# Second mixture of experts: outputs scattered from slots to tokens instead of gathered by token, and the last batch routed in the attention's stage

## The chip, the core and the metric

The kernel runs on one core of a Trainium2 chip. A core has five engines with a queue of instructions each: TensorE (PE in the profile, its weight loads PEld), VectorE (DVE), ScalarE (ACT), GpSimd (POOL) and SyncE (SP). Each engine takes its instructions strictly in order. Transfers are issued by SP, by ACT and, where the rows are chosen by an index tile, by POOL; all of them run on the core's 16 DMA engines. The metric is the device time of the core in microseconds, the median of several runs.

## The reference, cut to what matters

The input is x with 8 batches of 512 tokens of 128 numbers, 4096 tokens in all. There are two layers, each `x = x + s * silu(g)` over a layer norm of x. In the first, s is a state-space block (a scan over time for 16 states and 256 channels) and g a mixture of 24 experts with two matmuls each. In the second, s is a causal attention with 8 heads of width 128, and g is the second mixture, which this change is about:

```python
logits = xt @ wg                      # 4096 tokens, 128 experts
gates = softmax(logits)
e1, e2 = the two best experts         # loc1, loc2: the token's place in each one's list
g1, g2 = g1 / (g1 + g2), g2 / (g1 + g2)
v1, v2 = loc1 < 32, loc2 < 32         # an expert has 32 places; later comers are dropped
buf[e1 * 32 + loc1] += xt * v1        # second choices come behind all first choices
buf[e2 * 32 + loc2] += xt * v2
yb = einsum('ecd,edf->ecf', buf, we)  # one 128x128 matmul for each expert
y = (g1 * v1) * yb[place of e1] + (g2 * v2) * yb[place of e2]
```

A token that is dropped by an expert gets nothing from it.

## The kernel before

All instructions are written in Python loops. A scheduler then sets each engine's order: it takes ready instructions by their place in the program, and lets later ones go ahead while earlier ones wait. Semaphore waits follow from which tiles (also those in DRAM) an instruction reads and writes. Tiles with the same tag share a fixed number of buffers, so a new tile waits until an old one is released.

**The stages.** First come the preparation of x, the routing of the first mixture, and its experts; the scan runs beside them in steps (`step`, 64 in all, each two of the 16 states of one batch, with `front` and `back` for what goes in and comes out). Then the *early* attention stage follows: batches 0 to 5, 8 heads each, 48 in all (`early`), with the scan's remaining steps spread evenly over the 48. `back(b)` writes `s_dram[b]`, which `fetch(b)` loads; `after(b, ...)` makes the second layer's input of it, and `Attention.prepare(b, xb)` the layer norm, the logits, the two best experts, the attention's input and, in `route`, the places.

**Routing.** For each token and choice k the index `e * 32 + place` goes into `idx1` (a dropped token gets a spare row past 4096). Each batch has four tiles of 128 tokens, and each tile is stored twice by an indirect DMA of POOL (line 831), into `xs_dram[0]` for the first choice and `xs_dram[1]` for the second. Both tables were filled with zeros near the start of the program (line 415).

**The late stage.** When the early heads and the scan are through, their pools are given up and new ones are opened, PSUM among them. In program order there follow batch 7's `after` and `prepare`, `weights2` (weights of all tokens), `places` (which slots of the second choice's half hold a token: `live`, from the expert counts), and then batches 6 and 7's heads. Between these 16 heads stand the second mixture's pieces: `slots(t)` loads 512 slots of each table and transposes them; `experts(e0, ...)` does eight experts' matmuls, multiplies by `live` and stores the slots' outputs into `yb_dram` (line 979); and `finish(b)` for batches 0 to 5. Batches 6 and 7's `finish` comes at the end. `finish(b)` loads s1 and x1, gathers for each of four token tiles the rows of the first and second expert (lines 991 and 992, through the helper at line 127), weights and adds them (lines 993 and 994), and stores the result. Batches of s1, x1 and y have two buffers each; the gathered rows share six; the experts' output `yb` has three.

The lines that the change and the prediction speak of most:

```python
G.indirect_dma_start(xs_dram[k][:, :], IOA(idx1[:, b * NJ + j, k : k + 1], 0), xn2[:, j, :], None)   # 831
V.tensor_tensor(yb, py, bc(live[:, e0 // 2 : e0 // 2 + 4].unsqueeze(2), (P, 4, D)), ALU.mult)        # 978
Q.dma_start(rows(yb_dram[2 * C1 * e0 : 2 * C1 * (e0 + 8), :]), yb)                                   # 979
```

Other lines named: 605 to 608 are the scan on VectorE, 629 its transposes on TensorE; 849 to 863 a head's scores and exponentials (859 adds the mask and takes the minimum), 877 to 895 its values.

Of the kernel before, what the change touches and what calls it, by code (L numbers as in the profile page):

```python
# [20 lines left out]
P = 128  # L21
# [11 lines left out]
S1 = E1 * C1  # L33
HEADS, DHEAD = 8, 128
# [12 lines left out]
def tile_kernel(ctx: ExitStack, tc: tile.TileContext, t: dict, out: bass.AP):  # L47
# [42 lines left out]

    xs_dram = [dram.tile([S1 + P, D], F32, name=f"xs_dram{k}") for k in range(2)]
    yb_dram = dram.tile([2 * S1, D], F32, name="yb_dram")

# [75 lines left out]
    w121 = w3.tile([P, NTT, 2], F32, name="w121")  # L169
    row1 = w3.tile([P, NTT, 2], I32, name="row1")  # L170
    idx1 = w3.tile([P, NTT, 2], I32, name="idx1")
    kp1 = w3.tile([P, NTT, 2], F32, name="kp1")
# [22 lines left out]
    zero = inv_pool.tile([P, L], F32, name="zero")  # L195
    G.memset(zero, 0.0)
# [140 lines left out]
    def routing():  # L337
# [75 lines left out]
        for k in range(2):  # L413
            tc.keep_in_program_order(
                Q.dma_start(
                    xs_dram[k][0:S1, :].rearrange("(p n r) d -> p n (r d)", p=P, r=L // D),
                    bc(zero.unsqueeze(1), (P, S1 // L, L)),
                )
            )
# [323 lines left out]
    class Attention:  # L743
# [6 lines left out]
        def prepare(self, b, xb):  # L750

            at, (ps_x, px) = self.at, self.ps_x
            xn2 = at.tile([P, NJ, D], F32, name="xn2", bufs=1)
            layernorm(st, xb, xn2, NJ, eps5, "ln1")
            pt = ps_x.tile([P, L], F32, name="pt2", tag=px)
            for j in range(NJ):
                T.transpose(pt[:, j * P : (j + 1) * P], xn2[:, j, :], ident)
# [12 lines left out]
            V.tensor_tensor(lg, lg, bc(mx1[:, bs, 0:1], (P, NJ, E1)), ALU.subtract)  # L770
            S.activation(lg, lg, AF.Exp)
            V.tensor_reduce(se1[:, bs], lg, AX.X, ALU.add)

            sq = at.tile([P, NJ, D], F32, name="sq2", bufs=1)
            ss = st.tile([P, NJ], F32, name="ss2")
            for j in range(NJ):
                S.activation(sq[:, j, :], xn2[:, j, :], AF.Square, accum_out=ss[:, j : j + 1])
# [4 lines left out]
            V.tensor_tensor(sq, xn2, bc(ss.unsqueeze(2), (P, NJ, D)), ALU.mult)  # L782
            pt = ps_x.tile([P, L], F32, name="pt3", tag=px)
            for j in range(NJ):
                T.transpose(pt[:, j * P : (j + 1) * P], sq[:, j, :], ident)
            xaT = at.tile([P, L], F32, name="xaT", bufs=3)
            S.activation(xaT, pt, AF.Copy, scale=gamma)
            self.route(b, xn2)
            return xaT

        def route(self, b, xn2):
# [28 lines left out]
            kp = kp1[:, bs, :]  # L820
# [5 lines left out]
            for k in range(2):  # L826
                V.tensor_scalar(pos[:, :, k], pos[:, :, k], float(C1 - 1), float(k * C1), ALU.min, ALU.add)
            V.scalar_tensor_tensor(row1[:, bs, :], e12, float(2 * C1), pos, ALU.mult, ALU.add)
# [87 lines left out]
    def weights2():  # L916
        V.reciprocal(se1, se1)
        V.tensor_tensor(w121, mx1[:, :, 0:2], bc(mx1[:, :, 0:1], (P, NTT, 2)), ALU.subtract)
        S.activation(w121, w121, AF.Exp)
        V.tensor_tensor(w121, w121, bc(se1.unsqueeze(2), (P, NTT, 2)), ALU.mult)  # L920
        den = r3.tile([P, NTT], F32, name="den1")
        V.tensor_tensor(den, w121[:, :, 0], w121[:, :, 1], ALU.add)
        V.tensor_scalar(den, den, EPS32, None, ALU.max)
        V.reciprocal(den, den)
        V.tensor_tensor(w121, w121, bc(den.unsqueeze(2), (P, NTT, 2)), ALU.mult)
        V.tensor_tensor(w121, w121, kp1, ALU.mult)

    def places():


        pair = r3.tile([P, 2], F32, name="pair")
# [19 lines left out]
        V.tensor_scalar(live, pk, c, float(C1), ALU.add, ALU.is_lt)  # L951


    def slots(t):
        for k in range(2):
            xg = mo.tile([P, 4, D], F32, name="xg1", bufs=4)
            Q.dma_start(xg, rows(xs_dram[k][t * L : (t + 1) * L, :]))
            px = ps_x.tile([P, 4, P], F32, name="pxs", tag="px")
            for j in range(4):
                T.transpose(px[:, j, :], xg[:, j, :], ident)  # L960
# [11 lines left out]
    def experts(e0, we):  # L972
# [6 lines left out]
        Q.dma_start(rows(yb_dram[2 * C1 * e0 : 2 * C1 * (e0 + 8), :]), yb)  # L979

    def finish(b):
# [4 lines left out]
        y = mo.tile([P, NJ, D], F32, name="y", tag="y")  # L986
# [78 lines left out]
    for n, of in mixture():  # L1065
        due += n / of
        while due > 0.5:
            step()
            due -= 1.0
    moe.close()  # L1070
# [22 lines left out]
    def early():  # L1093
        for b in range(EARLY):
# [33 lines left out]
    live = r3.tile([P, E1 // 2], F32, name="live")  # L1128
    loaded = {e0: load_experts(e0) for e0 in range(0, 32, 8)}
# [21 lines left out]
    for b in range(EARLY):  # L1151
        second.append([lambda b=b: finish(b)])
# [5 lines left out]
    for b in range(EARLY, B):  # L1158
# [67 lines left out]
```

## Time and profile before

| | |
|---|---|
| three runs | 1612.73, 1624.30, 1623.59 us; median 1623.59 |
| the profiled execution | 1646.25 us |
| its span, first to last instruction | 1644.5 us |
| mean granted TensorE clock | 0.866 |
| busy: TensorE matmul, VectorE, ScalarE, GpSimd | 1243.5, 1256.5, 986.1, 588.6 us |
| indirect DMAs of POOL in routing (line 831) | 64, 1248 ns mean |
| last scan transposes (line 629) | 1376 us |
| last `s_dram` store of the scan (line 703) | 1421 us |
| routing of the last batch, scatters | 1459.8 to 1469.6 us |
| expert outputs `yb` (line 978) | 1478.2 to 1533.3 us |
| gathers of `finish` | 1536.3 to 1636.5 us |

A profile is one execution; its durations and its span belong together, and its own time is above the median of the runs. A row of a timeline has the start, the time it took, the engine, the line, the operation with output and inputs by name, and in brackets how long the engine stood idle before it and what ended that. A row of a table of stretches has a stretch, its length, each engine's busy time with its number of instructions, the granted clock, the DMA engines' busy share and GB/s. The chain of waits goes back from the last instruction to whatever released it.

### The profile page before, as it was taken

What the parts mean: (1) busy time and instruction counts of PE and PEld (TensorE: products, weight loads), DVE (VectorE), ACT (ScalarE), POOL (GpSimd) and SP (SyncE); (2) the same over time, 40 slices, a digit from 0 to 9 for tenths busy, and PEclk for the clock granted to TensorE, in tenths of its full rate; (3) what the DMA queues carried; (4) which work ended last, traced back from release to release, by engine and by line L of the source; (5) the groups of instructions that cost most, each with busy time, mean ns of one, the idle gap of its engine ahead of it and who ended that gap; (6) DMA issues with size and microseconds to landing.
All of it is one profiled execution on the core that took longest, in us unless ns stands there. A gap on an engine that the chain in (4) does not pass through costs nothing.

```text
span 1644.5 us, 20522 instructions
## 1 busy us (share of the span) xinstructions
PE 1243.5 (76%) x6797; PEld 873.5 (53%) x6797; DVE 1256.5 (76%) x2831; ACT 986.1 (60%) x1696; POOL 588.6 (36%) x502
## 2 busy tenths in 40 slices
PE   4787989311389988174888998889898899889764
PEld 2654455101377886151465665656656667567443
DVE  6558687679847866695999999999989896475454
ACT  2226778557567786364677768758567574552442
POOL 2016653565264440722253405730521111010455
PEclk9887999655589999576899999989989899999886
DMA  4438987677567863423142412421321200439133
GB/s 137 150 112 288 302 286 227 218 239 229 167 194 252 269 188 124 121 84 83 55 108 64 110 64 63 95 90 60 78 65 52 81 29 14 104 104 256 53 109 93
DMA packets 170668, 222.76 MB, mean 135 GB/s; under 512 B 15722, under 2 KB 115898, under 8 KB 170562
## 3 DMA queue, kind: packets, MB, share of 16 engines
q1 hardware_dynamic: 125634, 101.35, 19.8%
q10 hardware_dynamic: 18432, 67.12, 12.4%
q0 software_dynamic: 26496, 52.98, 12.1%
q8 instruction: 54, 0.88, 0.2%
q14 instruction: 52, 0.43, 0.1%
HBM read 163.52 MB, written 57.80 MB: 135 GB/s over the span
## 4 chain that ended last, share of the span: by engine, by line
PE 35%; DVE 33%; DMA 10%; issue 9%; ACT 7%; POOL 5%; another core or an unknown queue 1%; ACTq 0%; SPq 0%; DVEq 0%; POOLq 0%
DVE u L607 8%; PE po L884 5%; PE sc L857 4%; DVE u L605 4%; DVE u L608 4%; DVE sc L859 3%; PE py L629 3%; PE ph L453 2%; DMA hd<-hs_dram,row 2%; PE po L520 2%; DMA os_dram<-os 2%; DVE s L895 2%; PE pp L877 2%; PE pc L561 2%; PE pv L842 2%
## 5 line engine op out<-in xcount | busy, mean ns | idle before, releaser
L607 DVE TENSOR_TENSOR_SCAN u<-da,u 128x512 f32<-128x512 f32 x256 | 311.5, 1238 | 67.5 <-ACT da L603 47.9
L629 PE MATMUL py<-ident,u 128*128 128x128 f32 x1024 | 171.2, 306 | 159.7 <-DVE u L608 159.4
L629 PEld LDWEIGHTS py<-ident,u 128*128 128x128 f32 x1024 | 135.8, 158 | 201.1 <-DVE u L608 176.0
L884 PE MATMUL po<-v,pT 128*128 128x129 f32 x1280 | 189.1, 291 | 40.2 <-DVE s L895 27.0
L884 PEld LDWEIGHTS po<-v,pT 128*128 128x128 f32 x1280 | 171.3, 203 | 73.6 <-issue 29.8
L603 ACT ACTIVATE da<-dt,a_neg 128x512 f32<-128x512 f32 x256 | 175.7, 720 | 53.7 <-DVE u L607 51.5
L863 ACT ACTIVATE prob<-sc,mn 128x128 f32<-128x128 f32 (+3 forms) x256 | 130.5, 528 | 112.3 <-DVE mn L859 97.8
L857 PE MATMUL sc<-xaT,qm 128*128 128x128 f32 (+3 forms) x512 | 180.2, 461 | 13.8 <-ACT prob L863 9.9
L605 DVE TENSOR_TENSOR u<-bb,lp 128x1024 f32<-128x1024 f32 x128 | 155.0, 1228 | 16.0 <-DMA bb<-xd_dram 16.0
L608 DVE TENSOR_TENSOR u<-u,cb 128x1024 f32<-128x1024 f32 x128 | 158.1, 1235 | 1.1
L859 DVE CUSTOM_DVE_ANT_0 sc<-sc,mask 128x128 f32<-128x128 f32 (+3 forms) x256 | 125.2, 497 | 35.9 <-PE sc L857 28.1
L831 POOL DMA_INDIRECT xs_dram<-xn,idx x64 | 79.9, 1248 | 162.4 <-DVE idx L825 110.3
L877 PE MATMUL pp<-ident,prob 128*128 128x128 f32 x640 | 113.5, 286 | 30.6 <-DVE pT L879 19.7
L127 POOL DMA_INDIRECT xg<-xn_dram,inv x72 | 89.5, 1243 | 131.0 <-DVE lp L584 78.8
L130 POOL DMA_INDIRECT o<-os_dram,row x64 | 114.1, 1783 | 46.8 <-DMA o<-xn_dram 29.0
L877 PEld LDWEIGHTS pp<-ident,prob 128*128 128x128 f32 x640 | 80.8, 146 | 93.5 <-issue 43.1
L127 POOL DMA_INDIRECT hg<-hid_dram,inv x72 | 88.5, 1230 | 104.9 <-PE pht L515 51.5
L857 PEld LDWEIGHTS sc<-xaT,qm 128*128 128x128 f32 x512 | 82.8, 198 | 51.7 <-ACT prob L863 26.7
L127 POOL DMA_INDIRECT hd<-hs_dram,row x64 | 76.1, 1189 | 80.2 <-DMA bb<-xd_dram 31.6
L879 ACT COPY pT<-pp 128x384 f32<-128x384 f32 (+1 forms) x93 | 48.0, 516 | 57.8 <-PE pp L877 41.4
L520 PE MATMUL po<-we,hgT 128*128 128x128 f32 x576 | 79.7, 288 | 0.3 <-ACT hgT L517 0.3
L520 PEld LDWEIGHTS po<-we,hgT 128*128 128x128 f32 x576 | 72.3, 199 | 14.0 <-issue 9.8
(293 smaller groups left out, 2595.6 us busy)
## 6 DMA issues: line engine op xcount, KB each, us to landing
bb<-xd_dram ACTq DMA_DIRECT2D x64, 512.0 KB
cb<-xd_dram ACTq DMA_DIRECT2D x64, 512.0 KB
hs_dram<-hs SPq DMA_DIRECT2D x24, 768.0 KB
we<-in_W SPq DMA_DIRECT2D x48, 256.0 KB
hid_dram<-hd SPq DMA_DIRECT2D x32, 256.0 KB
we<-in_we SPq DMA_DIRECT2D x16, 512.0 KB
os_dram<-os SPq DMA_DIRECT2D x24, 192.0 KB
xb<-in_x SPq DMA_DIRECT2D x16, 256.0 KB
```

The source lines that it names most:

```text
L127: G.indirect_dma_start(dst, None, table[:, :], IOA(idx, 0))
L520: T.matmul(po[:, c, :], hT[:, f, :], we[:, f, :], start=False, stop=(f == NJ - 1))
L603: S.activation(da[:, j, :], dt[:, hf, :], AF.Exp, scale=a_neg[:, hf, n0 + j : n0 + j + 1])
L605: V.tensor_tensor(u, bb, bc(dx[:, hf : hf + 1, :], (P, NC, L)), ALU.mult)
L607: V.tensor_tensor_scan(u[:, j, :], da[:, j, :], u[:, j, :], 0.0, ALU.mult, ALU.add)
L608: V.tensor_tensor(u, u, cb, ALU.mult)
L629: T.matmul(py[:, i, hf * P : (hf + 1) * P], us[hf][:, j, i * P : (i + 1) * P], ident, is_transpose=True, start=False, stop=(n0 + j == DS - ...
L857: T.matmul(sc[:, :w], qm[:, i * P : w], xaT[:, :w], start=True, stop=True)
L859: V.tensor_tensor_reduce(sc[:, :w], sc[:, :w], mask[:, L - w :], -1.0, FMAX, ALU.add, ALU.min, mn[:, i : i + 1])
L863: S.activation(pr, sc[:, :w], AF.Exp, bias=mn[:, i : i + 1], scale=-1.0)
L877: T.transpose(pp[:, c, :], prob[i][:, k * P : (k + 1) * P], ident)
L884: T.matmul(po[:, i - i0, :], pT[:, i * (i + 1) // 2 + k, :], v[:, k, hd % 4, :], start=(k == 0), stop=(k == i),)
```

## The change

- The rows of both `xs_dram` tables grow from 128 to 132 numbers: behind the token's data stand, for each choice, its weight and its row in the output (`home`). They are filled not with zeros alone but with a spare output row for empty slots.
- `prepare` works out the batch's two weights itself (`weights2` goes) and puts them and `home` behind the normalised token, so that `route`'s scatters carry them along. `route` no longer computes the gather's rows.
- `places` loads weights and rows back from the tables by slot, multiplies `live` with the weights, and keeps the rows in `to`.
- `experts` stores its four tiles of slots by four indirect DMAs of POOL, straight to the tokens' rows of `y_dram`, which has one half for each choice. 16 calls make 64 of them. `y_dram` is filled with zeros behind the first mixture.
- `finish(b)` loads both halves' 512 rows and adds them; all eight `finish` come behind all heads.
- The scan's remaining steps are spread over 42 of the early heads, not 48, and batch 7's `fetch`, `after` and `prepare` are put between the last of the 48.

```diff
-    xs_dram = [dram.tile([S1 + P, D], F32, name=f"xs_dram{k}") for k in range(2)]
-    yb_dram = dram.tile([2 * S1, D], F32, name="yb_dram")
+    xs_dram = [dram.tile([S1 + P, DX], F32, name=f"xs_dram{k}") for k in range(2)]     # DX = D + 4
+    y_dram = dram.tile([2 * NY, D], F32, name="y_dram")                                # NY = NTOK + P
...
+    home_i = w3.tile([P, NTT + 1, 2], I32, name="home_i")
+    G.iota(home_i, pattern=[[P, NTT + 1], [NY, 2]], base=0, channel_multiplier=1)
...
-                    xs_dram[k][0:S1, :].rearrange("(p n r) d -> p n (r d)", p=P, r=L // D),
-                    bc(zero.unsqueeze(1), (P, S1 // L, L)),
+                    xs_dram[k][0:S1, :].rearrange("(p n) d -> p n d", p=P),
+                    bc(empty[:, k : k + 1, :], (P, S1 // P, DX)),
...
         def prepare(self, b, xb):
...
+            V.reciprocal(se1[:, bs], se1[:, bs])
+            w12 = st.tile([P, NJ, 2], F32, name="w121")
+            V.tensor_tensor(w12, mx1[:, bs, 0:2], bc(mx1[:, bs, 0:1], (P, NJ, 2)), ALU.subtract)
+            S.activation(w12, w12, AF.Exp)
+            V.tensor_tensor(w12, w12, bc(se1[:, bs].unsqueeze(2), (P, NJ, 2)), ALU.mult)
+            den = st.tile([P, NJ], F32, name="den1")
+            V.tensor_tensor(den, w12[:, :, 0], w12[:, :, 1], ALU.add)
+            V.tensor_scalar(den, den, EPS32, None, ALU.max)
+            V.reciprocal(den, den)
+            more = xn2[:, :, D:].rearrange("p j (k a) -> p j k a", a=2)
+            V.tensor_tensor(more[:, :, :, 0], w12, bc(den.unsqueeze(2), (P, NJ, 2)), ALU.mult)
+            V.tensor_copy(more[:, :, :, 1], home[:, bs, :])
...
         def route(self, b, xn2):
...
-            for k in range(2):
-                V.tensor_scalar(pos[:, :, k], pos[:, :, k], float(C1 - 1), float(k * C1), ALU.min, ALU.add)
-            V.scalar_tensor_tensor(row1[:, bs, :], e12, float(2 * C1), pos, ALU.mult, ALU.add)
...
     def places():
+        more = r3.tile([P, E1 // 2, 2], F32, name="more")
+        for a in range(2):
+            for k in range(2):
+                h = 2 * C1 * a + C1 * k
+                Q.dma_start(
+                    more[h : h + C1], xs_dram[k][0:S1, D + 2 * k : D + 2 * k + 2].rearrange(
+                        "(q a c) d -> a c q d", a=2, c=C1)[a]
+                )
...
+        V.tensor_tensor(live, live, more[:, :, 0], ALU.mult)
+        V.tensor_copy(to, more[:, :, 1])
...
     def experts(e0, we):
...
-        Q.dma_start(rows(yb_dram[2 * C1 * e0 : 2 * C1 * (e0 + 8), :]), yb)
+        for j in range(4):
+            q = e0 // 2 + j
+            G.indirect_dma_start(y_dram[:, :], IOA(to[:, q : q + 1], 0), yb[:, j, :], None)
...
     def finish(b):
...
-        for j in range(NJ):
-            i = b * NJ + j
-            ya = mo.tile([P, D], F32, name="ya", tag="row", bufs=6)
-            yc = mo.tile([P, D], F32, name="yc", tag="row", bufs=6)
-            gather(ya, yb_dram, row1[:, i, 0:1])
-            gather(yc, yb_dram, row1[:, i, 1:2])
-            V.tensor_scalar(ya, ya, w121[:, i, 0:1], None, ALU.mult)
-            V.scalar_tensor_tensor(y[:, j, :], yc, w121[:, i, 1:2], ya, ALU.mult, ALU.add)
+        y = mo.tile([P, NJ, D], F32, name="y")
+        Q.dma_start(y, rows(y_dram[b * L : (b + 1) * L, :]))
+        y2 = mo.tile([P, NJ, D], F32, name="y2")
+        Q.dma_start(y2, rows(y_dram[NY + b * L : NY + (b + 1) * L, :]))
+        V.tensor_tensor(y, y, y2, ALU.add)
...
+    for k in range(2):
+        tc.keep_in_program_order(
+            Q.dma_start(
+                y_dram[k * NY : k * NY + NTOK, :].rearrange("(p n) d -> p n d", p=P),
+                bc(empty[:, 0:1, 0:D], (P, NTOK // P, D)),
+            )
+        )
     moe.close()
...
     total = EARLY * HEADS
+    done = total - 6
...
-        while (taken - (NSTEP - left)) * total < (i + 1) * left:
+        while (taken - (NSTEP - left)) * done < (i + 1) * left and taken < NSTEP:
             step()
+        if i == done - 1:
+            for _ in model_steps:
+                pass
+        if i == done + 1:
+            got = fetch(B - 1)
+        if i == done + 2:
+            xb = after(B - 1, *got)
+            ready[B - 1] = beside.prepare(B - 1, xb)
...
-    for b in range(EARLY + 1, B):
-        ready[b] = last.prepare(b, after(b, *fetch(b)))
-    weights2()
     places()
...
-    for b in range(EARLY):
-        second.append([lambda b=b: finish(b)])
...
-    for b in range(EARLY, B):
+    for b in range(B):
         finish(b)
```

More of the change, by code (lines that the diff above doesn't have):

```diff
@@ L33 @@
 S1 = E1 * C1
+DX = D + 4
+NY = NTOK + P
 HEADS, DHEAD = 8, 128
@@ L168, in tile_kernel @@
     e121 = w3.tile([P, NTT, 2], F32, name="e121")
-    w121 = w3.tile([P, NTT, 2], F32, name="w121")
-    row1 = w3.tile([P, NTT, 2], I32, name="row1")
+    home = w3.tile([P, NTT + 1, 2], F32, name="home")
+    home_i = w3.tile([P, NTT + 1, 2], I32, name="home_i")
+    G.iota(home_i, pattern=[[P, NTT + 1], [NY, 2]], base=0, channel_multiplier=1)
+    V.tensor_copy(home, home_i)
     idx1 = w3.tile([P, NTT, 2], I32, name="idx1")
-    kp1 = w3.tile([P, NTT, 2], F32, name="kp1")
     cnt = w3.tile([NTT, 2, E1], BF16, name="cnt")
@@ L194, in tile_kernel @@
     bias = inv_pool.tile([3 * 32, DH + D], BF16, name="bias")
-    zero = inv_pool.tile([P, L], F32, name="zero")
-    G.memset(zero, 0.0)
+    empty = inv_pool.tile([P, 2, DX], F32, name="empty")
+    G.memset(empty, 0.0)
+    for k in range(2):
+        G.tensor_copy(empty[:, k, D + 2 * k + 1 : D + 2 * k + 2], home[:, NTT, k : k + 1])
     pick = inv_pool.tile([3 * 32, E0], BF16, name="pick")
@@ L752, in prepare @@
             at, (ps_x, px) = self.at, self.ps_x
-            xn2 = at.tile([P, NJ, D], F32, name="xn2", bufs=1)
-            layernorm(st, xb, xn2, NJ, eps5, "ln1")
+            xn2 = at.tile([P, NJ, DX], F32, name="xn2", bufs=1)
+            layernorm(st, xb, xn2[:, :, 0:D], NJ, eps5, "ln1")
             pt = ps_x.tile([P, L], F32, name="pt2", tag=px)
             for j in range(NJ):
-                T.transpose(pt[:, j * P : (j + 1) * P], xn2[:, j, :], ident)
+                T.transpose(pt[:, j * P : (j + 1) * P], xn2[:, j, 0:D], ident)
             xT = at.tile([P, L], F32, name="xT2", bufs=1)
@@ L776, in prepare @@
             for j in range(NJ):
-                S.activation(sq[:, j, :], xn2[:, j, :], AF.Square, accum_out=ss[:, j : j + 1])
+                S.activation(sq[:, j, :], xn2[:, j, 0:D], AF.Square, accum_out=ss[:, j : j + 1])
             V.tensor_scalar(ss, ss, 1e-24, None, ALU.max)
@@ L781, in prepare @@
             V.tensor_scalar(ss, ss, float(D) ** 0.5, None, ALU.mult)
-            V.tensor_tensor(sq, xn2, bc(ss.unsqueeze(2), (P, NJ, D)), ALU.mult)
+            V.tensor_tensor(sq, xn2[:, :, 0:D], bc(ss.unsqueeze(2), (P, NJ, D)), ALU.mult)
             pt = ps_x.tile([P, L], F32, name="pt3", tag=px)
@@ L819, in route @@
                 V.tensor_reduce(pos[:, j0 : j0 + 2, :], pm, AX.X, ALU.add)
-            kp = kp1[:, bs, :]
+            kp = st.tile([P, NJ, 2], F32, name="kp1")
             V.tensor_scalar(kp, pos, float(C1), None, ALU.is_lt)
@@ L913, in heads @@
                 yield
[L916 to L926, printed above, removed]
-    def places():
+    def places():
+        more = r3.tile([P, E1 // 2, 2], F32, name="more")
[6 more added lines that the diff above has]
+                )
         pair = r3.tile([P, 2], F32, name="pair")
@@ L951, in places @@
         V.tensor_scalar(live, pk, c, float(C1), ALU.add, ALU.is_lt)
+        V.tensor_tensor(live, live, more[:, :, 0], ALU.mult)
+        V.tensor_copy(to, more[:, :, 1])
     def slots(t):
         for k in range(2):
-            xg = mo.tile([P, 4, D], F32, name="xg1", bufs=4)
+            xg = mo.tile([P, 4, DX], F32, name="xg1", bufs=4)
             Q.dma_start(xg, rows(xs_dram[k][t * L : (t + 1) * L, :]))
@@ L959, in slots @@
             for j in range(4):
-                T.transpose(px[:, j, :], xg[:, j, :], ident)
+                T.transpose(px[:, j, :], xg[:, j, 0:D], ident)
             dst, src = xsT[:, 16 * t : 16 * t + 16, k, :], px.rearrange("p j (e c) -> p (j e) c", c=C1)
@@ L985, in finish @@
         Q.dma_start(x1, rows(x1_dram[b][:, :]))
-        y = mo.tile([P, NJ, D], F32, name="y", tag="y")
-        for j in range(NJ):
-            i = b * NJ + j
-            ya = mo.tile([P, D], F32, name="ya", tag="row", bufs=6)
-            yc = mo.tile([P, D], F32, name="yc", tag="row", bufs=6)
-            gather(ya, yb_dram, row1[:, i, 0:1])
-            gather(yc, yb_dram, row1[:, i, 1:2])
-            V.tensor_scalar(ya, ya, w121[:, i, 0:1], None, ALU.mult)
-            V.scalar_tensor_tensor(y[:, j, :], yc, w121[:, i, 1:2], ya, ALU.mult, ALU.add)
+        y = mo.tile([P, NJ, D], F32, name="y")
[3 more added lines that the diff above has]
+        V.tensor_tensor(y, y, y2, ALU.add)
         S.activation(y, y, AF.Silu)
@@ L1069, in tile_kernel @@
             due -= 1.0
+    for k in range(2):
+        tc.keep_in_program_order(
[4 more added lines that the diff above has]
+        )
     moe.close()
@@ L1128, in tile_kernel @@
     live = r3.tile([P, E1 // 2], F32, name="live")
+    to = r3.tile([P, E1 // 2], I32, name="to")
     loaded = {e0: load_experts(e0) for e0 in range(0, 32, 8)}
     last = Attention(at, m_qk, w_vo, (ps_x, "px"), (ps_q, "pq"), (ps_s, "ps"), (ps_t, "pt"), (ps_o, "po"))
-    for b in range(EARLY + 1, B):
-        ready[b] = last.prepare(b, after(b, *fetch(b)))
-    weights2()
     places()
```

## The prediction, made before the changed kernel ran

> **What bounds the kernel now.** The program has stages with different limits, so I read the table of stretches before anything else. The first stretch is the stage in which the scan shares the engines with the attention; the others cut what follows at the last scan work (1376), the first late head (1423), the last scatter of the routing (1471) and the last expert output (1533).
>
> ```profile
> core 0: us, PE busy (x) PEld busy (x) DVE busy (x) ACT busy (x) POOL busy (x), PEclk, DMA share, GB/s
> 790.00:1376.00 586.00, 525.19 (x2823) 365.28 (x2821) 554.01 (x1399) 411.33 (x705) 183.19 (x130) 0.94 0.24 70
> 1376.00:1423.00 47.00, 40.19 (x199) 26.07 (x198) 21.63 (x73) 23.38 (x49) 9.05 (x10) 0.96 0.08 23
> 1423.00:1471.00 48.00, 43.10 (x217) 28.65 (x216) 30.91 (x129) 27.90 (x57) 10.25 (x10) 0.96 0.51 133
> 1471.00:1533.00 62.00, 58.69 (x514) 45.42 (x513) 37.10 (x99) 21.39 (x42) 0.13 (x1) 1.00 0.72 204
> 1533.00:1645.00 112.00, 62.20 (x278) 43.91 (x276) 52.34 (x181) 42.73 (x66) 62.68 (x64) 0.76 0.32 90
> ```
>
> Up to 1376 VectorE is the bound: 554.0 of 586 us, 94.5%. After that no engine is full, so waits decide. How many attention heads each stretch holds is read from the mask-and-minimum line, L859, at 8 instructions a head:
>
> ```profile
> core 0: us, DVE busy (x), PEclk, DMA share, GB/s
> 790.00:1376.00 586.00, 98.99 (x368) 0.94 0.24 70
> 1376.00:1423.00 47.00, 5.20 (x20) 0.96 0.08 23
> 1423.00:1471.00 48.00, 10.33 (x38) 0.96 0.51 133
> 1471.00:1533.00 62.00, 10.54 (x38) 1.00 0.72 204
> 1533.00:1645.00 112.00, 13.32 (x48) 0.76 0.32 90
> ```
>
> That is 46, 2.5, 4.75, 4.75 and 6 heads. From 1376 to 1423 only two and a half remain from the early list, since the late heads need PSUM that the last `back` still holds. From 1423 a head takes 10.1 us; from 1471, with the experts between, 13.1; from 1533 about 17, since six batches' gathers sit in the same in-order queues. The waits and the chain of the end name what the last stretch hangs on:
>
> ```profile
> POOL ya L127 <- DMA yb_dram<-yb: 64.9, 1, 64.9
> 1533.30 2.27 DMA yb_dram<-yb
> ...
> 1635.60 3.06 DMA yc<-yb_dram,row
> ```
>
> The gathers start when the last expert's store has landed; the very last gather needs 3.06 us to land and is followed by 6 us of `finish`.
>
> **The row that decides the change** is the routing's scatter, L831, the only indirect store in the trace:
>
> ```profile
> 1310.30 1.86 POOL L831 DMA_INDIRECT xs_dram<-xn,idx  x1 [0.59 <-DVE rsum L889]
> 1312.47 0.97 POOL L831 DMA_INDIRECT xs_dram<-xn,idx  x1 [0.30 <-issue]
> 1315.50 1.02 POOL L831 DMA_INDIRECT xs_dram<-xn,idx  x1 [2.06 <-DMA xs_dram<-xn,idx]
> 1317.52 0.96 POOL L831 DMA_INDIRECT xs_dram<-xn,idx  x1 [1.01 <-DMA xs_dram<-xn,idx]
> ...
> 1461.05 0.97 POOL L831 DMA_INDIRECT xs_dram<-xn,idx  x1 [0.30 <-issue]
> 1462.32 0.96 POOL L831 DMA_INDIRECT xs_dram<-xn,idx  x1 [0.30 <-issue]
> 1463.59 0.95 POOL L831 DMA_INDIRECT xs_dram<-xn,idx  x1 [0.30 <-DMA xs_dram<-xn,idx]
> ```
>
> They alternate between two tables. The third waits until the first has landed, the fourth for the second: a scatter into a table waits for the scatter before it into the same table, since nobody knows the rows in advance. With two tables this hides at quiet times (1461.05 to 1463.59 is 2.54 us, two issues of 1.27). In the busy group it does not: 1310.30 to 1315.50 is 5.20, 1312.47 to 1317.52 is 5.05. The change sends all 64 output scatters into one table, `y_dram`, so every one waits for its predecessor.
>
> **Step 1, the scan stage.** The scan's steps are spread over 42 heads, not 48, so at its end six heads fewer are done, and batch 6's `after` and `prepare` still lie ahead. A head costs VectorE, by its groups over 64 heads, (125.2 + 36.5 + 68.6 + 9.8 + 58.4 + 21.1 + 21.0) / 64 = 5.3 us of summed durations, about 4.3 net because neighbours overlap; six are 26 us. `prepare` plus `after` is 14 us net (four 128x512 passes of 0.69, maxima and indices 2.4, masks 1.4, positions 3.1, two layer norms 4.5). So 40 us / 0.945 = 42 us earlier. Against it:
> - Eight small VectorE instructions more in each `prepare`, three fewer in `route`, each about 0.08 us net (0.16 by duration): 0.5 us for each of five batches, 2.5 us, on the bound engine. The eight exponentials go to ScalarE, 70% busy here: nothing, or 1.28 us for each table load they cause (ends 0 and 10 us; I take 0, as another exponential stands just before).
> - Two zero fills of `y_dram`, 4.2 MB of 512-byte rows on SP's queue at the start of the attention, where VectorE waits for the first gather-adds. At 306 GB/s (the best 20 us of such rows, 1480 to 1500) they take 14 us. All hidden is 0, none hidden 14; I take 4, as POOL's issue paces the gather-adds.
> - `xs_dram`'s fill in 528-byte pieces, not 2 KB: bounds -1 and 3 us, beside mixture work at 115 us; I take 2. The two memsets shrink: nothing.
>
> The scan ends at 1376 - 42 + 8 = **1342**.
>
> **Step 2, the last batch.** Moving its `prepare` forward can't start it sooner than `s_dram[7]`, which comes out of the last `back`. From scan end to the last routing scatter landed took 1376 to 1471, 95 us: `back` to 1421, load and `after` to 1436, `prepare` to 1459, eight scatters. The same chain stands in the changed kernel, now beside some eight early heads (VectorE work 34 + 28 + 8 us in 97) where there were 2.5 and 4.75. I take 98 (ends 90, with the `we` loads out of its way, and 110): **1440**. What the move does gain is that the hole of 1376 to 1423 is filled with heads.
>
> **Step 3, first output scatter.** `places` now loads weights and rows from `xs_dram`, four DMAs of 2048 pieces of 8 bytes ahead of the slot loads on SP. No row has such a load; below nothing it can't be, above I allow 15 us; nearest are the SP issues (0.36 us for 512 pieces), so 1.3 each: 5 us. Then 8 us as before (1471 to the first yb at 1479): **1453**.
>
> **Step 4, the chain of 64 scatters.** Issue 0.96, landing 2.1 to 2.3 us after the start when quiet, 0.27 to the next start: 2.5. All 64 routing scatters land after a median of 2.3 and a mean of 2.8 us; the late stage carries the slot and weight loads, some 90 GB/s, so I take 2.75 a step: 176 us, ending at **1629** (ends 2.45 and 3.4: 1610 and 1671). The Trainium skill, "DMA: Bandwidth & Descriptors", section "Anatomy of one DMA", gives 2.0 us + bytes / 436 GB/s for a DMA issued by GpSimd; 64 KB make 2.15 us, an estimate of 138 us and 1591. The row shows what this leaves out, the wait's release and the load of the queues, and it decides. The page also says that the fixed part is completion latency, longest towards HBM; that speaks against a change that puts 64 of them in a row.
>
> The heads hide beneath this: 16 from about 1430 at 9 to 10 us, and 21 us of experts and transposes on PE, end at 1595 to 1611. Behind a waiting scatter on POOL only `v`'s small memsets stand, behind a full `yb` (three buffers) VectorE's next head; that cover is 15 to 30 us thick.
>
> **Step 5, the finish.** All eight batches now come after the last scatter, since each reads `y_dram`. Per batch four loads and a store of 256 KB, 10.5 MB in all, of which 1 MB (s1, x1 of two batches) is loaded ahead: 31 us at 306 GB/s, 44 at 214 (1420 to 1440). By buffers: load 3, add, silu, multiply, add with hand-overs 3, store 2.3, for two batches at a time, 4 x 8.3 = 33. I take 38 (33 to 45) and 1 for the close: **1668**. Gone are 64 gathers (62.6 us of POOL) and 64 small VectorE operations (20 us); they lay in the stretch that is now heads alone.
>
> **Sum.** 1668 - 1644.5 = +23.5 us on the profiled span. Its execution took 1646.25, 1.75 around the span; the three runs have a median of 1623.59. I put the difference on the median: **1647 us**, 1.4% slower. A measurement of this kernel tells about 1% (16 us) from no change.
>
> **The rivals.**
> - *The chain at its floor, no real change.* 2.5 us x 64 = 160, step 2 in 92, finish 34: 1342 + 92 + 13 + 160 + 34 + 1 = 1642, -2.5: 1621 us. For it: the quiet group of 1459 to 1469. Against: loads run beside it. 0.22.
> - *Not slower at all, but faster:* the scatters don't hold one another up and run at POOL's 1.27 us. 64 are 81 us, so outputs are there by 1550, the heads end at 1600, and the finish of the first batches fills their gaps: 1600 + 13 = 1613, -31: 1592 us. The point is the step: with the rest as above the change pays below (1644.5 - 1453 - 39) / 64 = 2.38 us. Against it: the rows above. 0.17.
> - *Heavy queues and late experts.* The steps stay at 3.4 as in the group of 1310 (eight scatters, mean landing 3.2), or experts stand in PE's order behind heads and the chain starves: 218 us, finish 40: 1712, +67: 1690 us. 0.12.
> - My forecast: 0.49.
>
> **Range and chances.** The forecast's own range is 1633 to 1668. To leave out no more than two in ten it must take in the floor and part of the two ends: 1592 to 1690. Faster by over 1%: the second rival, 0.17. Within 1%: the floor, and 0.06 from the lower edge of the forecast, 0.28. Slower: the rest of the forecast and the third rival, 0.43 + 0.12 = 0.55.
>
> **What would show it.** Right: the `y_dram` scatters start one by one, 2.5 to 3 us apart, each "<-DMA y_dram<-yb,to"; the last scan line ends near 1342; heads end well ahead of the last scatter; then some 38 us with a high DMA share, PE empty. Wrong: scatters 1.27 apart (the chain is no chain), heads ending after the last scatter, routing's last scatter far from 1440, or a finish interleaved with heads.

## The result and the profile after

The changed kernel takes **1713.3 us** (median of four runs, 1711.5 to 1715.9) where the kernel before takes 1622.0 beside it: a ratio of **1.058 (95% interval 1.0545 to 1.0617)**, slower by 91 us. The forecast was 1647. The profiled execution took 1711.7 us with a span of 1710.0, 65.5 more than the span of the page before.

The table of stretches, cut where the forecast's steps end: scan end, the routing of batches 6 and 7, first output scatter, last head, last output scatter landed. Columns are the stretch, its length, busy time (instructions) of PE, its weight loads, VectorE, ScalarE and POOL, the granted clock, the DMA share and GB/s.

```profile
core 0: us, PE busy (x) PEld busy (x) DVE busy (x) ACT busy (x) POOL busy (x), PEclk, DMA share, GB/s
790.00:1342.00 552.00, 472.94 (x2565) 330.26 (x2564) 511.43 (x1272) 368.83 (x642) 171.86 (x122) 0.94 0.26 73
1342.00:1390.00 48.00, 41.36 (x217) 28.00 (x216) 30.44 (x105) 35.11 (x70) 8.46 (x8) 0.96 0.06 18
1390.00:1432.00 42.00, 25.00 (x133) 18.43 (x131) 20.43 (x88) 12.61 (x23) 9.41 (x10) 0.76 0.57 146
1432.00:1467.00 35.00, 25.51 (x95) 14.90 (x96) 19.10 (x76) 14.32 (x31) 8.62 (x9) 0.66 0.07 20
1467.00:1482.00 15.00, 13.36 (x83) 9.13 (x82) 7.66 (x25) 5.75 (x12) 0.59 (x2) 1.00 0.79 137
1482.00:1560.00 78.00, 68.90 (x466) 49.81 (x467) 34.74 (x110) 30.98 (x60) 24.58 (x27) 0.96 0.37 106
1560.00:1641.00 81.00, 72.47 (x466) 51.28 (x461) 39.56 (x133) 36.30 (x69) 28.10 (x30) 1.00 0.10 32
1641.00:1664.00 23.00, 0.00 (x0) 0.00 (x0) 0.71 (x3) 0.00 (x0) 8.28 (x9) 0.56 0.11 37
1664.00:1710.00 46.00, 0.00 (x0) 0.00 (x0) 15.82 (x24) 5.04 (x8) 0.00 (x0) 0.50 0.71 206
```

The first row is nearly as busy on VectorE as before (511.4 of 552 us, 93%, where it was 94.5%). From 1390 to 1467 PE has 50.5 us of work in 77: that hole is new. From 1641 PE has nothing at all: 69 us of the program contain only scatters and then `finish`. Two rows of the waits (engine and line, releaser: us in total, times, longest) say what these ends hang on:

```profile
POOL y_dram L997 <- DMA y_dram<-yb,to: 116.4, 62, 4.3
DVE y L1008 <- DMA y<-y_dram: 40.8, 4, 26.1
```

Of 63 scatters that follow another one, 62 waited for the one before (the other one is put down to VectorE). POOL's own order of time shows the routing and the start of that chain (start, duration, instruction, idle time before it and its releaser):

```profile
1423.02 1.01 POOL L848 DMA_INDIRECT xs_dram<-xn,idx  x1 [20.99 <-DVE idx L845]
...
1432.26 0.96 POOL L848 DMA_INDIRECT xs_dram<-xn,idx  x1 [0.32 <-DMA xs_dram<-xn,idx]
1455.31 0.96 POOL L848 DMA_INDIRECT xs_dram<-xn,idx  x1 [22.10 <-DVE idx L845]
...
1464.21 0.96 POOL L848 DMA_INDIRECT xs_dram<-xn,idx  x1 [0.30 <-DMA xs_dram<-xn,idx]
1471.69 0.13 POOL L856 MEMSET v<- 128x16 f32 x1 [6.52 <-PE po L901]
1481.54 0.96 POOL L997 DMA_INDIRECT y_dram<-yb,to  x1 [9.72 <-DVE mn L876]
...
1614.73 0.96 POOL L997 DMA_INDIRECT y_dram<-yb,to  x1 [1.52 <-DMA y_dram<-yb,to]
1617.23 0.96 POOL L997 DMA_INDIRECT y_dram<-yb,to  x1 [1.54 <-DMA y_dram<-yb,to]
1619.71 0.96 POOL L997 DMA_INDIRECT y_dram<-yb,to  x1 [1.53 <-DMA y_dram<-yb,to]
1622.69 0.96 POOL L997 DMA_INDIRECT y_dram<-yb,to  x1 [2.02 <-DMA y_dram<-yb,to]
```

Batch 7's eight scatters start at 1455, only 23 us after batch 6's are out, although VectorE had begun on its input at 1395. The start of batch 7's layer norm, and what VectorE waited for before its end:

```profile
1395.08 0.49 DVE L109 BATCH_NORM_STATS2 ln_st<-xb 128x6 f32<-128x128 f32 x2 [3.30 <-POOL xb L553]
...
1434.66 1.11 DVE L119 TENSOR_SCALAR xn<-xb,ln_mv,ln_rs 128x128 f32<-128x128 f32 x4 [11.91 <-DMA xs_dram<-xn,idx]
```

The second row writes `xn2`. That tile has one buffer, and it is the source of batch 6's scatters: it is free when the last of these has landed.

The heads are counted as before, at eight instructions each on the mask line (now L876):

```profile
core 0: us, DVE busy (x), PEclk, DMA share, GB/s
1343.00:1467.00 124.00, 17.49 (x64) 0.81 0.24 62
1467.00:1642.00 175.00, 35.48 (x128) 0.98 0.28 74
```

Eight heads in the 124 us after the scan, and 16 left at 1467. The kernel before had 10.75 left at 1471 (86 instructions).

The tail, in VectorE's order of time and in the chain that ended last:

```profile
1667.87 0.69 DVE L1008 TENSOR_TENSOR y<-y,y 128x512 f32<-128x512 f32 x1 [26.13 <-DMA y<-y_dram]
1680.62 1.45 DVE L1008 TENSOR_TENSOR y<-y,y 128x512 f32<-128x512 f32 x2 [7.15 <-DMA y<-y_dram]
1690.66 0.69 DVE L1008 TENSOR_TENSOR y<-y,y 128x512 f32<-128x512 f32 x1 [5.91 <-DMA y<-y_dram]
1701.26 0.69 DVE L1008 TENSOR_TENSOR y<-y,y 128x512 f32<-128x512 f32 x1 [5.80 <-DMA x1f<-x_dram]
```

```profile
1672.90 3.91 DMA out<-y
1676.83 3.67 DMA y<-y_dram
```

Two batches take 10 to 13 us, since the next load of `y` waits until the store out of the same buffer has landed.

### The profile page after: what moved, and what is told of

Its sections match the earlier page's. It is cut to its first block, busy times and chain, and to the rows that moved or that the text cites. A ratio compares the mean times of both kernels' runs of the same rounds, so it can differ in the third digit from the quotient of the medians.

```text
span 1710.0 us, 20505 instructions
## 1 busy us (share of the span) xinstructions
PE 1231.5 (72%) x6797; PEld 865.7 (51%) x6797; DVE 1248.0 (73%) x2799; ACT 962.1 (56%) x1690; POOL 597.1 (35%) x505
## 4 chain that ended last, share of the span: by engine, by line
DVE 27%; PE 20%; DMA 18%; issue 7%; POOL 7%; ACT 3%; SPq 0%; DVEq 0%; ACTq 0%; POOLq 0%
DMA y_dram<-yb,to 9%; DVE u L614 6%; PE po L901 3%; DVE u L612 3%; POOL o L133 3%; PE sc L874 3%; DVE u L615 3%; PE po L527 2%; DVE sc L876 2%; DMA xs_dram<-xn,idx 2%; DMA hd<-hs_dram,row 2%; DMA os_dram<-os 2%; PE py L636 2%; POOL hd L130 1%; DVE s L912 1%
## 5 line engine op out<-in xcount | busy, mean ns | idle before, releaser
L636 PE MATMUL py<-ident,u 128*128 128x128 f32 x1024 | 166.5, 300 | 134.4 <-DVE u L615 134.3
L901 PE MATMUL po<-v,pT 128*128 128x129 f32 x1280 | 185.2, 288 | 11.7 <-DVE s L912 7.7
L901 PEld LDWEIGHTS po<-v,pT 128*128 128x128 f32 x1280 | 167.2, 200 | 39.4 <-issue 13.9
L876 DVE CUSTOM_DVE_ANT_0 sc<-sc,mask 128x128 f32<-128x128 f32 (+3 forms) x256 | 124.6, 496 | 43.8 <-PE sc L874 42.0
L130 POOL DMA_INDIRECT xg<-xn_dram,inv x72 | 96.0, 1334 | 135.1 <-DVE lp L591 80.1
L130 POOL DMA_INDIRECT hg<-hid_dram,inv x72 | 93.4, 1298 | 86.7 <-PE pht L522 34.1
L997 POOL DMA_INDIRECT y_dram<-yb,to x64 | 61.3, 958 | 129.4 <-DMA y_dram<-yb,to 116.4
L859 PE MATMUL pv<-w_vo,xaT 128*128 128x512 f32 x128 | 69.8, 644 | 15.7 <-DVE zm L708 9.2
L896 ACT COPY pT<-pp 128x384 f32<-128x384 f32 (+1 forms) x106 | 54.9, 518 | 45.2 <-PE pp L894 44.0
```

What stands on the lines that cost most here:

```text
L130: G.indirect_dma_start(dst, None, table[:, :], IOA(idx, 0))
L636: T.matmul(py[:, i, hf * P : (hf + 1) * P], us[hf][:, j, i * P : (i + 1) * P], ident, is_transpose=True, start=False, stop=(n0 + j == DS - ...
L876: V.tensor_tensor_reduce(sc[:, :w], sc[:, :w], mask[:, L - w :], -1.0, FMAX, ALU.add, ALU.min, mn[:, i : i + 1])
L901: T.matmul(po[:, i - i0, :], pT[:, i * (i + 1) // 2 + k, :], v[:, k, hd % 4, :], start=(k == 0), stop=(k == i),)
```

## The experiments

The kernel before is not equally fast on every chip: it took 1619 to 1622 us in two of the comparisons and 1645 to 1649 in the three others, which were on three different chips. The changed kernel was measured beside both kinds and took nearly the same (1713 and 1716). So each result below names the time of the kernel before on its chip, and times are compared on like chips, except where the text says otherwise. The terms of the sum, each read from that kernel's trace, in us:

| | whole change | again | scatters only | two `xn2` | two tables, half | tail buffers | both mended |
|---|---|---|---|---|---|---|---|
| scan's last step | 1343.2 | 1349.8 | 1382.8 | 1348.6 | 1341.0 | 1346.4 | 1340.8 |
| to the last routing scatter | 121.0 | 120.3 | 94.6 | 98.9 | 121.2 | 121.2 | 98.8 |
| to the first output scatter | 17.3 | 18.1 | 15.3 | 20.0 | 17.3 | 17.4 | 17.5 |
| to the last output scatter | 180.2 | 178.3 | 185.6 | 179.0 | 113.0 | 180.4 | 178.1 |
| to the end of the span | 48.3 | 47.8 | 47.9 | 47.7 | 61.5 | 39.0 | 38.6 |
| late heads end at | 1641.8 | 1648.0 | 1609.8 | 1626.5 | 1644.0 | 1645.4 | 1615.3 |
| span | 1710.0 | 1714.3 | 1726.2 | 1694.2 | 1654.1 | 1704.3 | 1673.8 |

**The scatters without the move.**

```diff
-    done = total - 6
+    done = total
...
-        if i == done - 1:
...
-            ready[B - 1] = beside.prepare(B - 1, xb)
...
+    for b in range(EARLY + 1, B):
+        ready[b] = last.prepare(b, after(b, *fetch(b)))
     places()
```

> Half of the change: outputs scattered to tokens, but the last batch prepared in the late stage as before. Theory (the chain of dependent scatters ends the program, and the move of the last batch bought nothing): routing's last scatter near 1469 as before, first output scatter near 1484, 64 steps of 2.85 us = 182, last one landed near 1667, tail 46, span near 1713: the same time as the whole change within 10 us. Rival (what costs is the move, which leaves 16 heads to do at 1467 where before had 10.75 at 1471): the heads end near 1600, and the span is 1650 to 1665, some 50 us below the whole change.

Measured: 1723.8 us, before 1618.6 on this chip, ratio 1.063 (1.0595 to 1.0664). In its table of stretches:

```profile
1493.00:1610.00 117.00, 96.08 (x654) 71.11 (x652) 50.89 (x159) 39.97 (x77) 35.89 (x38) 0.93 0.30 83
1610.00:1681.00 71.00, 6.18 (x40) 4.58 (x40) 3.46 (x5) 1.87 (x2) 25.77 (x27) 0.52 0.09 29
1681.00:1726.00 45.00, 0.00 (x0) 0.00 (x0) 15.83 (x24) 5.04 (x8) 0.00 (x0) 0.50 0.73 210
```

The heads end at 1610 as the rival said, and it gains nothing: in the 71 us in which the chain runs out PE has 6.2 us of work left. The span is 1726.2 where the theory had 1713, and the loss is 105 us, more than the whole change's 91: chain and tail alone are enough for it.

**The move without the scatters.** The kernel before with the change's last three hunks (the pace of 42 heads, batch 7 between the early heads).

> The other half: gathers by token and weights as before, but the last batch routed in the attention's stage, with the scan spread over 42 heads. Theory (the move loses time by itself, because the last two batches' routing now runs one behind the other after the scan): last routing scatter at 1460 to 1467, about as before, some 15 heads left there instead of 10.75; at 62 us for the experts' stretch (4.75 heads), then 17 us a head beside the gathers and 10 after them, span 1665 to 1695 against 1644.5, 1 to 3 per cent slower. Rival (the move fills the hole of 1376 to 1423 and is a gain by itself, eaten by the scatters): 1 per cent faster than before, span near 1625.

Measured: 1674.2 us, before 1618.6, ratio 1.0326 (1.029 to 1.0362): slower by 56 us. Its span of 1673.2 lies within the theory's 1665 to 1695; the per cent of the theory (1 to 3) were reckoned from the page of 1644.5, and on this chip they are 3.3. Its last routing scatter starts at 1465.1, 112 us after its scan ends. The heads, again by the mask line (here L859):

```profile
1467.00:1571.00 104.00, 22.29 (x80) 1.00 0.43 124
1571.00:1664.00 93.00, 12.93 (x48) 0.85 0.37 101
```

Ten heads in 104 us beside the experts, six in 93 beside the gathers. 16 heads are left at 1467, and the program ends 10 us after they do. The two parts don't add up (105 and 56 us, together 91): with the scatters the move's extra heads lie beneath the chain, and the routing comes forward from 1477 to 1464, which fits the 10 us that separate 1723.8 from 1713.3.

**Two buffers for `xn2`.**

```diff
-            xn2 = at.tile([P, NJ, DX], F32, name="xn2", bufs=1)
+            xn2 = at.tile([P, NJ, DX], F32, name="xn2", bufs=2)
```

> The whole change with two buffers for xn2 instead of one, so that the last batch's prepare needn't wait until the scatters of batch 6 have landed (VectorE stood 11.9 us, PE 14.3 us for that). Theory (the routing's end sets the start of the chain and of the late heads): last routing scatter 12 us earlier (8 to 25), everything after it as much earlier, time 12 us (8 to 25) below the whole change. Rival (the order of the in-order queues holds it, the buffer is only the last of several waits): under 4 us.

Measured: 1686.7 us, before 1618.6, ratio 1.0391 (1.0346 to 1.0437): 27 us below the whole change on a like chip. POOL's order of time:

```profile
1432.67 0.96 POOL L848 DMA_INDIRECT xs_dram<-xn,idx  x1 [0.33 <-DMA xs_dram<-xn,idx]
1438.51 0.95 POOL L848 DMA_INDIRECT xs_dram<-xn,idx  x1 [4.88 <-DVE idx L845]
...
1447.53 0.96 POOL L848 DMA_INDIRECT xs_dram<-xn,idx  x1 [0.30 <-DMA xs_dram<-xn,idx]
```

Batch 7's scatters now follow batch 6's after 5 us instead of 23. The stretch from scan end to the last routing scatter falls from 121 to 98.9 us. In this profile, the slowest of its four runs (1675.7 to 1695.9), the chain starts 14 us earlier than in the whole change and the span is 16 us shorter. The buffer was the wait. The gain is just beyond the 8 to 25 us expected: the 12 us put first counted only VectorE's idle time, not all of the `prepare` that could run earlier.

**Two tables, half of the outputs.**

```diff
-            G.indirect_dma_start(y_dram[:, :], IOA(to[:, q : q + 1], 0), yb[:, j, :], None)
+            G.indirect_dma_start(y_drams[j % 2][:, :], IOA(to[:, q : q + 1], 0), yb[:, j, :], None)
```

> The whole change with the output scatters alternating between two tables; finish reads only the first table, so half of the expert outputs are left out of the sum, and finish moves the same bytes as in the whole change. Theory (each scatter waits for the one before into the same table): steps fall from 2.85 to 1.3 to 1.6 us, the last scatter comes 80 to 100 us after the first, near 1575, the heads end last, near 1625 to 1640, and the tail of 35 to 45 us follows: span 1665 to 1685, 25 to 45 us below the whole change. Rival 1 (the step is the price of a scatter into rows of 512 bytes, not a wait for the table): steps stay at 2.5 or more and the time is the same. Rival 2 (the scatters are hidden beneath the heads anyway): steps fall, the time falls by under 10 us.

Measured: 1659.4 us, before 1618.6, ratio 1.0255 (1.0216 to 1.0294): 54 us below the whole change. The row of its waits, and a stretch of POOL's order of time:

```profile
POOL y_dram L997 <- DMA y_dram<-yb,to: 29.4, 34, 3.2
```

```profile
1570.14 0.96 POOL L997 DMA_INDIRECT y_dram<-yb,to  x1 [0.75 <-DMA y_dram<-yb,to]
1571.40 0.95 POOL L997 DMA_INDIRECT y_dram<-yb,to  x1 [0.30 <-issue]
1572.67 0.96 POOL L997 DMA_INDIRECT y_dram<-yb,to  x1 [0.32 <-DMA y_dram<-yb,to]
1573.93 0.96 POOL L997 DMA_INDIRECT y_dram<-yb,to  x1 [0.30 <-DMA y_dram<-yb,to]
```

The same 64 scatters of the same rows go at 1.26 us in a group: the step was a wait for the table, not the price of a scatter. The chain falls to 113 us (more than the expected 80 to 100; 17.4 us of POOL's waits within it end with VectorE, which makes the outputs between the heads), the heads end last, at 1644.0, and `finish` runs beneath them: 10 us remain behind the last head, not the expected 35 to 45, so the time is also below the expected 1665 to 1685. What is left, 41 us above before, fits the move's 16 heads, on which this version ends.

**Tail buffers.** Four buffers for `y` and `x1`, three for `y2` and `s1`, where each had two.

> The whole change with four buffers for y and x1 and three for y2 and s1 in finish, instead of two each. Theory (the tail of 46 us is paced by its ring of two buffers: load, add, silu, multiply, add, store landed, and only then the next load, 10.6 to 12.7 us for each two batches): the tail falls to 30 to 36 us, time 10 to 16 us below the whole change. Rival (the bytes pace it, 206 GB/s is what these rows get): tail 43 or more, under 4 us.

Measured: 1710.3 us, before 1644.6, ratio 1.0414 (1.0366 to 1.0461). Beside the changed kernel on a like chip (1716.0, below) that is 6 us; the intervals overlap. In the traces the tail from the last scatter's start falls from 48 to 39.0 us, just short of the 10 expected, and it does so again in the run with both terms mended (38.6): the ring of two buffers did pace it.

**The changed kernel again, and the kernel before again.**

> The changed kernel once more, on the chip of the next three kernels. On one chip the kernel before takes 1619 us, on another 1645; the page of before came at 1646, the page of the changed kernel at 1712. Theory (the chips differ in what before waits for and hardly in the changed kernel's chain): 1705 to 1725 us wherever it runs, ratio 1.058 where before takes 1620, 1.04 where it takes 1645. Rival (the slower chip is slower for both): 1737 us there, ratio 1.058 on either.

Measured: 1716.0 us, before 1646.2 on this chip, ratio 1.0436 (1.0392 to 1.048). As the theory said, the two comparisons differ in what before takes, and hardly in the changed kernel.

> The kernel before once more, for a second profile: the first profiled execution took 1646.25 us where the runs have a median near 1620, while the other kernels' profiled executions lie within 8 us of their medians. Theory (that execution was a slow draw, by some 25 us): a profiled time of 1612 to 1630, with the scan ending 10 to 25 us earlier than 1376 or the last stretch shorter than 112 us. Rival (this program is slower whenever it is profiled): 1640 to 1650 again.

Measured: 1642.2 us, and its runs there have a median of 1644.6. The rival's number came, but its reading fell with the theory's: on this chip 1645 is the program's usual time, profiled or not. The page of before, at 1646, fits such a chip and not the one of the runs beside it.

**Both mended, one table.** Two buffers for `xn2` and the tail's buffers together.

> The whole change, one table, with both mended terms at once: two buffers for xn2, and four buffers for y and x1, three for y2 and s1. Theory (the span is a sum of terms in a row: scan end, routing, chain of 64, tail): routing's last scatter 17 to 20 us earlier than in the change, chain unchanged at 181 to 185, tail 37 to 40, together 26 to 34 us below the change as measured on the same or any chip, 1680 to 1690 us. Rival (the terms overlap, the heads take over as the end): under 20 us.

Measured: 1674.6 us, before 1649.4, ratio 1.0166 (1.013 to 1.0202), 41 us below the changed kernel's 1716.0 on a like chip and more than the 26 to 34 expected. By the pages, 1673.8 against 1710.0, the 36.2 us are: scan -2.4, routing -22.2, start of the chain +0.2, chain -2.1, tail -9.7. The terms stand in a row and add up. Its late stretches:

```profile
1457.00:1616.00 159.00, 144.01 (x932) 103.53 (x930) 75.50 (x244) 68.07 (x130) 53.76 (x57) 0.97 0.24 69
1616.00:1637.00 21.00, 0.00 (x0) 0.00 (x0) 0.00 (x0) 0.00 (x0) 7.66 (x8) 0.53 0.11 37
1637.00:1674.00 37.00, 0.00 (x0) 0.00 (x0) 15.98 (x24) 5.01 (x8) 0.00 (x0) 0.50 0.84 234
```

The heads still end 21 us ahead of the chain, and the tail's DMA share is up from 0.71 to 0.84.

> The kernel before a third time, for the place where it loses 25 us on some chips. Theory (only its waits for transfers differ): if it takes about 1620 us here, the scan still ends at 1370 to 1376 and the gathers' stretch of 112 us is 15 to 25 us shorter; rival (VectorE's stage itself is shorter): the scan ends at 1350 to 1357. If it takes about 1645 us again, nothing is told apart.

Measured: 1650.7 us, scan end 1377.9. This was a chip of the slower kind again, so nothing is told apart.

**In search of a version that beats both.** Scatters into two tables in turn with all four loads added, once with batch 7 late, once with the move and two `xn2`:

> Scatters to tokens into two tables in turn, all four loads added in finish, the last batch prepared in the late stage as before, the finishes of six batches between the late heads. Theory (with the chain halved the heads set the end, as they did before, without 64 gathers beside them): steps near 1.5 us, last output scatter near 1590, heads end near 1605, 10 to 20 us of finish, 1605 to 1630 us, from 1 per cent faster than before to the same. Rival (another limit stands there: 4 MB more to fill and 4 MB more to load, and adds on VectorE): 1640 to 1665 us, 1 to 3 per cent slower than before.

> The same two tables, all four loads added, but with the last batch routed in the attention's stage as in the change, and two buffers for xn2. Theory (the move leaves 14 to 16 heads at 1450 to 1467, which is more than the late stage with the experts can do by the time the old order ends): heads end near 1625 to 1635, 1635 to 1655 us, slower than the two tables with the late prepare by 15 to 40 us. Rival (the move pays once the chain is short): faster than the two tables with the late prepare.

Measured: late 1678.9 us (ratio 1.0196, 1.0142 to 1.0249), moved **1647.8** (1.0018, 0.9999 to 1.0037), before 1644.6. Their per cents show that both forecasts were reckoned from a before of some 1620 us, so the ratios decide. The late one is 2.0% slower, as its rival said, not the same or 1% faster. The moved one came within its 1635 to 1655, but where before takes 1645, so it is as fast as before; and it is 31 us faster than the late one, not slower, as its own rival said (it has the second `xn2` buffer besides). From the last output scatter to the end it takes 65.8 and 71.2 us; the moved one has its last scatter at 1579, the late one at 1616. The stretch of the moved one, and two steps of its chain of waits:

```profile
1580.00:1650.00 70.00, 46.13 (x231) 33.33 (x230) 46.79 (x123) 35.72 (x56) 0.05 (x1) 0.82 0.69 200
```

```profile
1640.45 2.27 DMA s_dram<-s
1642.73 2.75 DMA s1f<-s_dram
```

Seven transfers of 256 KB for each batch, less the 1 MB loaded ahead, are 13.6 MB, and 70 us at 200 GB/s are 14.0. The chain went from 180 to 118 us, and the second table's loads stand behind it. But the heads still matter in the moved one: they end at 1640.4, and its last 10 us are the last head's store, the load of it and its `finish`. In the late one they end at 1650.7, and 31 us of `finish` follow. No run takes the loads and the heads apart here.

Then the order of the two prepares was attacked: the scan spread over 39 heads (or 36), batch 6's `prepare` right behind it, two `xn2`; with gathers as before (`move9`), and with two tables:

```diff
-    done = total - 6
+    done = total - 9
...
+        if i == done:
+            ready[B - 2] = beside.prepare(B - 2, after(B - 2, *fetch(B - 2)))
```

> Gathers by token as before. The last batch routed in the attention's stage, but with the scan spread over 39 heads instead of 42, batch 6's prepare right after the scan's last step in program order, and two buffers for xn2. Theory (the move loses in move_only because the two prepares run in a row behind the last back, and only some 8 heads fit into the 120 us between the scan's end and the routing's end): scan end near 1330, last routing scatter near 1430, all after it 25 to 35 us ahead of move_only: 1640 to 1655 us where before takes 1619. Rival (the gathers beside 16 heads hold the end, whatever comes before): within 8 us of move_only, 1666 to 1680.

> Scatters into two tables in turn, all four loads added, finishes between the late heads, and the scan spread over 39 heads with batch 6's prepare right after it; two buffers for xn2, three for x1. Theory (the heads now set the end, and what counts is how many of them fill the time between scan end and routing end): 10 to 16 us below two_tables_move, 0.6 to 1 per cent faster than before. Rival (the scan's steps, crowded among fewer heads, only push the early heads back): the same as before or slower, ratio 1.00 to 1.01.

> As early9, but with the scan spread over 36 heads, so that 12 early heads are left when it ends. Theory (100 us between scan end and routing end hold nine or ten heads; more of them only wait): within 5 us of early9. Rival (each head taken out of the scan's stage brings the routing and the experts another 4.5 us forward): another 10 to 14 us faster than early9.

Measured, before 1646.2 on this chip: `move9` 1659.0 (1.007, 1.0045 to 1.0095), two tables with 9 heads a ratio of 1.0056 (1.0029 to 1.0082), with 12 heads 1684.9 (1.0227, 1.0195 to 1.0259). `move9` has its last routing scatter at 1417.5, 48 us ahead of the move alone. How much of that it keeps is open, as the two ran on different kinds of chip: its span is 14 us shorter (1659.2 against 1673.2), its ratio 2.6 points lower, which is some 42 us. By its time it stands between its theory and its rival; by its ratio it is better than the theory (1640 to 1655 beside 1619). With 9 heads the rival's ratio of 1.00 to 1.01 came, and with 12 heads neither reading did: it is slower still. There the first output scatter comes 75 us behind the last of the routing, where it was 17, and PE is full of heads in between; the first row has its busy times, the second the mask line, ten heads of it:

```profile
1430.00:1506.00 76.00, 74.15 (x446) 53.68 (x447) 41.23 (x150) 39.96 (x80) 1.66 (x4) 1.00 0.16 28
1430.00:1506.00 76.00, 21.76 (x80) 1.00 0.16 28
```

The heads that were taken out of the scan's stage stand ahead of the experts in PE's order; the last output scatter starts at 1620, and 70 us follow again. No version here beats the kernel before.

## Why the prediction was too low

The direction was right, and so was the mechanism of the end: a chain of scatters that wait for one another, and a `finish` that can only come behind it. What failed is step 2, which copied the routing's length from before, and the base to which the sum was added. The forecast was 66 us too low, and it falls into two parts: 42 us in the sum (span 1710.0 against 1668) and some 24 in the base.

- **Step 1, scan end at 1342: right in sum.** It is 1343.2 (1349.8 in a second profile). With the scan over 48 heads it ends at 1382.8, which is 7 us behind the 1376 of before, where the additions had been put at 8. The move without the additions ends its scan at 1352.6, later than with them, so the 42 us and the 8 are not confirmed one by one.
- **Step 2, routing done at 1440: wrong by 26 us, the largest term.** The last scatter landed at 1466.5, 123 us behind the scan's end and not 98. The step said that "the same chain stands in the changed kernel" and copied its length. In the kernel before, batch 6's scatters (1382 to 1391) lay beside the last `back`; here batch 6's `prepare` itself falls behind the scan's end, with its scatters at 1423, and batch 7's stands behind it for the one `xn2`. The edit's program order puts both `prepare` behind the same early head. The step had both as VectorE work (28 us, twice the 14 of step 1), but not as two in line for one buffer. With two buffers the stretch is 98.9 us, with landing 101, against the 98 of the step. "Routing's last scatter far from 1440" was one of the prediction's own signs of being wrong. Why batch 6's layer norm, through at 1354, is followed by its transposes only at 1398 was not tried; the last `back` and the heads, which share PE and PSUM with it, are the likely reason.
- **Step 3, 13 us to the first scatter: 15.** The four loads of 8-byte pieces were issued in 4.1 us and landed 3.1 to 4.2 us after issue.
- **Step 4, 176 us of chain: 182.4** (180.2 and 2.2 to land). The quiet step is 2.49 us as worked out. The mean is 180.2 / 63 = 2.86, for two reasons. The first scatter of every group of four waits for VectorE and for its predecessor; the trace has a separate waiting instruction before it, and the step is 2.98 us, 0.5 longer (the 2.02 in the row of 1622.69). And beside the weight and slot loads, up to 1570, single steps took up to 5.25. The figure that the prediction took from the Trainium skill, "DMA: Bandwidth & Descriptors", section "Anatomy of one DMA", 2.0 us + bytes / 436 GB/s, holds for one landing (2.15 estimated, median 2.24 measured) and not for the chain (138 against 182).
- **The heads beneath it: right in length, late in start.** They were to end at 1595 to 1611 and ended at 1642, since they too start behind the routing: 16 heads and the experts took 175 us. The cover of 15 to 30 us was 22.
- **Step 5, 39 us of tail: 46.** The hand-over of a buffer from one pair of batches to the next was put at 8.3 us and took 10 to 13. With more buffers the stretch behind landing is 36.4.
- **The base.** "I put the difference on the median" took a page of 1646.25 and runs of 1623.59 for the same thing; 1647 is what the page itself shows for the kernel before. On chips where before takes 1645 the changed kernel takes 1716, a difference of 70 us, which is near the 65.5 of the two pages; beside runs of 1622 it is 91. What makes before 25 us slower on some chips, and leaves the changed kernel as it is, stays open. The mean granted clock of before is 0.874 (median of its runs) where it takes 1619 and 0.869 to 0.871 on the three slower chips; whether that is a cause or a mark of the longer time no run here shows.

With the two mis-sized terms mended the kernel is 1673.8 - 1649.0 = 24.8 us of span slower than before on the same chip, where the sum had said 23.5. Of the rivals, "the scatters don't hold one another up" fell with 62 waits of 63. The third one's span, 1712, lies beside the 1710 measured, but by luck: it had steps of 3.4 us and a chain of 218 from an early routing, and there came steps of 2.86 and a chain of 182 behind a late one.

## What to carry to other kernels

Where waits are set by the tile that an instruction writes, as here, stores by index into one table run one at a time, each a full landing behind the last (2.49 us a step; whether they could do without these waits was not tried); count the table's stores before the rows, and see what work must lie behind the last one. When a step is moved, follow its buffers as well as its inputs: a tile that a transfer reads is free only when that transfer has landed, and two copies of a step that never met before may now stand in line for it. Make the sum on a page and a median from the same chip.

## What the runs showed of the hardware that was not expected

- A scatter of 128 rows of 512 bytes lands 2.2 us after its start and frees the next into its table at 2.49; into two tables in turn the scatters of a group start every 1.26 us. A scatter with a second thing to wait for has an instruction of its own before it, and starts 2.98 us behind its predecessor instead of 2.49.
- One and the same program took about 1620 us in two comparisons and 1645 to 1649 in three others, on three chips, while the changed kernel took 1713 and 1716 beside either kind.
- A tail of loads and stores with rows of 512 bytes moved 200 to 234 GB/s; with more buffers for its tiles the whole change's tail went from 206 to 234.
